# Expert-choice routing on Trainium2: scales spread through memory, the eight largest found chunk by chunk, table rows in another order

## The chip, the cores and the metric

The kernel runs on one core of a Trainium2 chip. The core has five engines that run side by side: TensorE (PE in the profile; PEld is its weight load), VectorE (DVE), ScalarE (ACT), GpSimd (POOL) and SyncE (SP), which only issues DMAs here. The metric is the device time of one execution in microseconds. Ten runs of the kernel before gave a median of 6127.88 us (6120.04 to 6132.37).

## The reference, cut to what matters

The kernel computes a whole small vision model: four layers, each with a convolution-like block and a feed-forward block, on an activation of 4 images x 128 channels x 64 x 64 pixels. The change is in the feed-forward block that layers 1 and 2 share, a mixture of experts in which each of 64 experts chooses 8 of the 4096 tokens of an image:

```python
t = _to_tokens(x)                                  # 4 images, 4096 tokens, 128 channels
t = t + _L1_ffn_ref(_ln_t(t), ...)                 # the norm is over the channels of a token

logits = jnp.einsum('bsd,ed->bse', x, gate_w) + gate_b
probs = jax.nn.softmax(logits, axis=1)             # over the tokens
vals, idx = jax.lax.top_k(probs.transpose(0, 2, 1), K)      # K = 8, for each image and expert
gathered = jnp.take_along_axis(x, flat_idx[:, :, None], axis=1)
pooled = jnp.einsum('bked,bke->bed', gathered, topv)
h = gelu(h @ weight1); out = h @ weight2           # per expert, on the pooled row
outputs = outputs.at[..., flat_idx].add(weighted)  # back to the chosen tokens
```

## The kernel before

The activation stays in on-chip memory as `xs`, channels on the 128 partitions and tokens along the free dimension, in chunks of 512 tokens (eight chunks an image). The function `expert_choice` runs once for layer 1 and once for layer 2. It handles the four images as two pairs; a pair fills the 128 partitions of the logits (64 experts of each image). Its first half, which the change touches, is the selection:

- `stat(p, j)` (L1313, L1315, L1323): a product with the centring matrix, its square on ACT, and for each four chunks products that add up the variances into one bank `pv`, one row per chunk. `scales` and `inverted` (L1336, L1340) make 1/sqrt of them in one tile `rstd`: 16 useful rows of 512 tokens, a row for each chunk of the pair.
- `turn_scales` (L1346, L1348) turns these rows, so that a token's scale stands beside the token's row; the result is `turned`.
- `logits(p, c)` (L1357 to L1365): PE spreads the chunk's scale over the 128 partitions by a product with a selection matrix `own`, ACT copies it out, PE makes the logits with the centred gate, DVE multiplies the two, ACT adds the gate's bias. The result is the chunk's part of `chosen[p]`, 128 x 4096.
- `largest(p)` (L1398 to L1407): DVE finds the eight largest of the 4096 (MAX8), then their places (FIND_INDEX8), adds the image's offset and makes whole numbers of them.
- `rows(b, c)` (L1387 to L1392): four transposes turn 512 tokens into rows, ACT copies them into one of five buffers `xts`, adds the scale as one more column (L1390), and SP writes the buffer to a table in memory. The buffer's number is `(b * NCH + c) % len(xts)`, and the copy into a buffer waits until the write from it is done.
- `exponentials(p, c)`, `denominators(p)` (L1415, L1419, L1420): the softmax's sums.
- `ask(p, j)` (L1425): POOL asks by indirect DMA for the j-th chosen row of each expert from the pair's table.
- `pool(p)` (L1434 to L1452): diagonal matrices with the shares on DVE, eight products that pool the rows, a copy on ACT, the centring product, and a copy to `pooled`.

After that come the experts: 16 groups of four, whose weights (2 MB a group) are loaded by SP in order, four groups early, the rest as buffers come free. L1518 is their first product.

In this half PE, ACT, DVE and POOL work their instructions in the order of the program text (the pool of the stage is opened with `tc.manual_schedule(engines=ORDERED)`); only SP's DMAs are ordered by the scheduler. So an instruction that waits holds all that stand behind it on its engine. The order is written at the end of the stage:

```python
for c in range(NCH):
    logits(1, c)
    if c < 4:
        exponentials(0, c + 4)
    for n in (2 * c, 2 * c + 1):
        rows(1 + n // NCH, n % NCH)
denominators(0)
largest(1)
for c in range(NCH):
    rows(3, c)
    ask(0, c)
```

Of the kernel before, what the change touches and what calls it, by code (L numbers as in the profile page):

```python
# [28 lines left out]
P = 128  # L29
B, H, W = 4, 64, 64  # L30
N = H * W
CH = 512
NCH = N // CH
# [1182 lines left out]
def expert_choice(net, layer):  # L1216
# [24 lines left out]
    with ExitStack() as ctx:  # L1241
        dram = ctx.enter_context(tc.tile_pool(name="moe_dram", bufs=1, space=bass.MemoryType.DRAM))
        tables = [dram.tile([2 * N, ROW], F32, name=f"moe_table{p}") for p in range(PAIRS)]
        keep = ctx.enter_context(tc.tile_pool(name="moe", bufs=1))
        early = ctx.enter_context(tc.tile_pool(name="moe_w", bufs=EARLY))
        gate = keep.tile([D, E], F32, name="moe_gate")
# [18 lines left out]
        totals = [keep.tile([P, 1], F32, name=f"moe_total{i}") for i in range(PAIRS)]  # L1265
        cgate = keep.tile([D, E], F32, name="moe_cgate")

        behind = keep.tile([P, 1], F32, name="moe_behind")
        nc.gpsimd.memset(behind[0:E], 0.0)
        nc.gpsimd.memset(behind[E:P], float(N))  # L1270

        tops = {}
        negs = [keep.tile([P, 1], F32, name=f"moe_neg{p}") for p in range(PAIRS)]
# [22 lines left out]
        with (  # L1296
# [5 lines left out]
            def bank(tag, name):  # L1302
                return ps.tile([P, CH], F32, name=f"moe_{name}", tag=tag, bufs={"a": 3, "b": 3}.get(tag, 1))
# [28 lines left out]

            def scales(p):
                variances(p, 3)
                rstd = sb.tile([P, CH], F32, name="moe_rstd", tag="moe_rstd")
                nc.scalar.activation(rstd, stats[p][0], AF.Sqrt, bias=net.eps[1e-5])  # L1336
                rstds[p] = rstd

            def inverted(p):
                nc.vector.reciprocal(rstds[p], rstds[p])  # L1340

            def turn_scales(p):

                pt = bank("a", "pr")
                for k in range(4):
                    nc.tensor.transpose(pt[:, k * P : (k + 1) * P], rstds[p][:, k * P : (k + 1) * P], net.ident)  # L1346
                turned[p] = sb.tile([P, 2, NCH, 4], F32, name="moe_turned", tag="moe_turned")
                nc.vector.tensor_copy(  # L1348
                    turned[p].rearrange("p i (a q) k -> p k q (i a)", q=4),
                    pt.rearrange("p (k q r) -> p k q r", q=4, r=32)[:, :, :, 0:4],  # L1350
                )

            def logits(p, c):
                pb, pl = bank("b", "rb"), bank("a", "pl")
                q = c % 4
                rows = slice(32 * q, 32 * q + 32)
                nc.tensor.matmul(pb, own[rows, c // 4, :], rstds[p][rows], start=True, stop=True)  # L1357
                for i in range(2):
                    nc.tensor.matmul(
                        pl[i * E : (i + 1) * E], cgate, net.chunk(2 * p + i, c), start=True, stop=True  # L1360
                    )
                lg = chosen[p][:, c * CH : (c + 1) * CH]
                nc.scalar.copy(lg, pb)
                nc.vector.tensor_mul(lg, lg, pl)
                nc.scalar.activation(lg, lg, AF.Identity, bias=gbias)  # L1365

            xts = [sb.tile([P, 4, ROW], F32, name=f"moe_xt{i}", bufs=1) for i in range(5)]
            for t in xts:
                nc.gpsimd.memset(t[:, :, P:ROW], 0.0)

            own = sb.tile([P, 2, 2 * E], F32, name="moe_own", bufs=1)
            for q in range(4):
                group = slice(32 * q, 32 * q + 32)
                for r in range(2):
                    for i in range(2):
                        at = 32 * q + 2 * i + r
                        nc.gpsimd.tensor_copy(
                            own[group, r, i * E : (i + 1) * E], net.ident[group, at : at + 1].to_broadcast([32, E])
                        )

            def rows(b, c):

                p, i = divmod(b, 2)
                pt = bank("b", "pt")
                for t in range(4):
                    tok = slice((4 * c + t) * P, (4 * c + t + 1) * P)
                    nc.tensor.transpose(pt[:, t * P : (t + 1) * P], net.xs[:, b, tok], net.ident)  # L1387
                xt = xts[(b * NCH + c) % len(xts)]
                nc.scalar.copy(xt[:, :, 0:P], pt.rearrange("p (t d) -> p t d", d=P))
                nc.scalar.copy(xt[:, :, P], turned[p][:, i, c, :])  # L1390
# [3 lines left out]
            places, shares, asked = {}, {}, {}  # L1394

            def largest(p):
                top = keep.tile([P, K], F32, name=f"moe_top{p}")
                nc.vector.max(out=top, in_=chosen[p])  # L1398
                tops[p] = top
                place = sb.tile([P, K], U32, name="moe_place", tag="moe_place")  # L1400
                nc.vector.max_index(out=place, in_max=top, in_values=chosen[p])
                row = sb.tile([P, K], F32, name="moe_row", tag="moe_row")
                nc.vector.tensor_copy(row, place)
                nc.vector.tensor_scalar(row, row, behind, None, op0=ALU.add)
                places[p] = sb.tile([P, K], I32, name="moe_idx", tag="moe_idx")
                nc.vector.tensor_copy(places[p], row)
                nc.vector.tensor_scalar_mul(negs[p], top[:, 0:1], -1.0)  # L1407

            sums = [sb.tile([P, NCH], F32, name=f"moe_sums{p}", bufs=1) for p in range(PAIRS)]

            def exponentials(p, c):

                sq = sb.tile([P, CH], F32, name="moe_sq", tag="moe_sq", bufs=5)
                lg = chosen[p][:, c * CH : (c + 1) * CH]
                nc.scalar.activation(sq, lg, AF.Exp, bias=negs[p], accum_out=sums[p][:, c : c + 1])  # L1415

            def denominators(p):
                shares[p] = sb.tile([P, K], F32, name="moe_share", tag="moe_share")
                nc.scalar.activation(shares[p], tops[p], AF.Exp, bias=negs[p])  # L1419
                nc.vector.tensor_reduce(totals[p], sums[p], AX.X, ALU.add)  # L1420

            def ask(p, j):
                if j == 0:
                    asked[p] = sb.tile([P, K, ROW], F32, name="moe_asked", tag="moe_asked")
                nc.gpsimd.indirect_dma_start(  # L1425
                    out=asked[p][:, j, :],
                    out_offset=None,
                    in_=tables[p],
                    in_offset=bass.IndirectOffsetOnAxis(ap=places[p][:, j : j + 1], axis=0),
                )  # L1430
# [26 lines left out]
                stat(0, j)  # L1457
            scales(0)
            inverted(0)
            for j in range(5):  # L1460
                stat(1, j)
            turn_scales(0)
            pg = bank("b", "pg")
            nc.tensor.matmul(pg[:, 0:E], net.cent, gate, start=True, stop=True)
            nc.vector.tensor_copy(cgate, pg[:, 0:E])
            for c in range(NCH):
                logits(0, c)
            largest(0)
            for j in range(5, 2 * NCH):
                stat(1, j)  # L1470
                if j % 3 == 0:
                    rows(0, j // 3 - 2)
            scales(1)
            inverted(1)
            for c in range(4, NCH):
                rows(0, c)
                exponentials(0, c - 4)
            turn_scales(1)
            for c in range(NCH):
                logits(1, c)  # L1480
                if c < 4:
                    exponentials(0, c + 4)
                for n in (2 * c, 2 * c + 1):
                    rows(1 + n // NCH, n % NCH)
            denominators(0)
            largest(1)
            for c in range(NCH):
                rows(3, c)
                ask(0, c)
# [5 lines left out]
            pool(0)  # L1495

            pg = bank("b", "pb").rearrange("p (i c) -> p i c", i=NH)
            for i in range(NH):
# [1084 lines left out]
```

## Time and profile before

| what | value |
|---|---|
| median of ten runs | 6127.88 us |
| the profiled execution's own time | 6131.45 us |
| its span, first to last instruction | 6129.6 us |
| busy: PE, DVE, ACT, POOL | 5707.2, 4356.0, 3405.8, 2066.2 us |
| mean granted TensorE clock | 0.97 |
| bytes moved by DMA, mean rate | 836.40 MB, 136 GB/s |
| selection in layer 1, from the end of the first pair's variances to the experts' first product | 2500.70 to 2601.71 us |
| the same in layer 2 | 2970.14 to 3070.48 us |

Times in the views are microseconds from the start of the span unless they are marked ns. A timeline line gives start, duration, engine, source line, operation, output and inputs; where the engine stood idle before, a bracket at its end gives for how long and what released it. SPq is SP's queue of DMA issues.

### The profile page before, as it was taken

What the parts mean: (1) busy time and instruction counts of PE and PEld (TensorE: products, weight loads), DVE (VectorE), ACT (ScalarE), POOL (GpSimd) and SP (SyncE); (2) the same over time, 40 slices, a digit from 0 to 9 for tenths busy, and PEclk for the clock granted to TensorE, in tenths of its full rate; (3) what the DMA queues carried; (4) which work ended last, traced back from release to release, by engine and by line L of the source; (5) the groups of instructions that cost most, each with busy time, mean ns of one, the idle gap of its engine ahead of it and who ended that gap; (6) DMA issues with size and microseconds to landing.
All of it is one profiled execution on the core that took longest, in us unless ns stands there. A gap on an engine that the chain in (4) does not pass through costs nothing. (4 is left out here: it accounts for less than half of the span.)

```text
span 6129.6 us, 97925 instructions
## 1 busy us (share of the span) xinstructions
PE 5707.2 (93%) x39892; PEld 2243.1 (37%) x39923; DVE 4356.0 (71%) x4707; ACT 3405.8 (56%) x4256; POOL 2066.2 (34%) x2015
## 2 busy tenths in 40 slices
PE   8999999879999988789879999999999999999799
PEld 2222222446766766333333222322232223222233
DVE  6888887456767666357347778777877778888666
ACT  4444444332323222420428889888888888999421
POOL 3889896027777777100101111111111111111000
PEclk9999999989999999889989999999999999999899
DMA  6443431068777877440365566556665666666200
GB/s 212 97 84 78 97 77 41 1 189 251 225 242 231 257 215 211 149 162 0 125 234 125 131 149 146 126 130 144 142 135 123 140 140 138 132 136 131 62 23 28
DMA packets 291041, 836.40 MB, mean 136 GB/s; under 512 B 43356, under 2 KB 117596, under 8 KB 244492
## 3 DMA queue, kind: packets, MB, share of 16 engines
q0 software_dynamic: 109568, 505.75, 34.5%
q1 hardware_dynamic: 181004, 324.17, 18.2%
q8 instruction: 321, 5.26, 0.3%
q14 instruction: 148, 1.21, 0.1%
HBM read 416.71 MB, written 111.10 MB: 86 GB/s over the span
## 5 line engine op out<-in xcount | busy, mean ns | idle before, releaser
L1989 ACT ACTIVATE att_ex<-att_sc,att_shift 128x1024 f32<-128x1024 f32 x2048 | 2155.6, 1111 | 327.9 <-PE att_sc L1985 151.1
L2020 DVE TENSOR_TENSOR att_dve<-att_dve,att_ex 128x2048 f32<-128x2048 f32 x704 | 1633.8, 2321 | 348.8 <-ACT att_ex L1989 325.9
L1985 PE MATMUL att_sc<-att_q,att_k 32*128 32x512 f32 x8192 | 1283.8, 644 | 16.3 <-ACT att_ex L1989 16.3
L2001 PE MATMUL att_pv<-att_ex,att_vals 128*32 128x512 f32 x8192 | 1098.9, 608 | 6.6 <-ACT att_hidden L2027 5.6
L969 POOL DMA_INDIRECT dcn_g<-dcn_table,dcn_idx x896 | 850.2, 949 | 368.4 <-issue 156.3
L412 DVE SCALAR_TENSOR_TENSOR inv_prod<-inv_pk,bspan,inv_seen 128x512 f32<-128x512 f32 (+1 forms) x1120 | 774.6, 743 | 141.2 <-PE inv_pk L399 140.8
L410 POOL TENSOR_TENSOR inv_prod<-inv_seen,inv_prod 128x512 f32<-128x512 f32 (+1 forms) x672 | 837.6, 1274 | 95.0 <-ACT inv_prod L409 95.0
L2018 POOL DMA_DIRECT2D att_dma<-att_ex x224 | 192.5, 859 | 1912.8 <-ACT att_ex L1989 1681.1
L409 ACT ACTIVATE inv_prod<-inv_pk,bspan 128x512 f32<-128x512 f32 (+1 forms) x672 | 436.1, 682 | 504.7 <-PE inv_pk L399 494.9
L977 DVE TENSOR_TENSOR dcn_g<-dcn_g,dcn_near_w 128x1024 f32<-128x1024 f32 x448 | 540.0, 1216 | 217.7 <-DMA dcn_g<-dcn_table,dcn_idx 199.8
L1985 PEld LDWEIGHTS att_sc<-att_q,att_k 32*128 32x128 f32 x8192 | 423.5, 184 | 662.7 <-issue 436.6
L986 PE MATMUL dcn_pt<-ident,dcn_g 128*128 128x128 f32 x3584 | 479.3, 278 | 63.1 <-DVE dcn_g L977 39.0
L399 PE MATMUL inv_pk<-inv_red,wtap 32*96 32x512 f32 (+1 forms) x3584 | 511.8, 636 | 7.3 <-DVE wtap L377 7.3
L986 PEld LDWEIGHTS dcn_pt<-ident,dcn_g 128*128 128x128 f32 x3584 | 419.9, 143 | 222.4 <-issue 132.1
L421 PE MATMUL inv_out<-inv_prod,inv_fold 96*32 96x512 f32 (+1 forms) x3584 | 478.5, 606 | 8.5 <-DVE xs L429 8.5
L2001 PEld LDWEIGHTS att_pv<-att_ex,att_vals 128*32 128x32 f32 x8192 | 161.7, 108 | 793.6 <-issue 757.2
L1092 ACT COPY dcn_st<-dcn_pt 128x512 f32<-128x512 f32 x224 | 129.6, 579 | 307.8 <-PE dcn_pt L986 300.4
L399 PEld LDWEIGHTS inv_pk<-inv_red,wtap 32*96 32x96 f32 (+1 forms) x3584 | 131.6, 170 | 386.4 <-DVE inv_prod L412 362.7
L1099 PE MATMUL dcn_out<-dcn_st,dcn_wk 128*128 128x512 f32 x448 | 237.6, 613 | 24.1 <-DVE xs L1107 21.7
L2487 PE MATMUL top_po<-top_xg,top_we 128*128 128x512 f32 x512 | 233.5, 599 | 0.0
L1005 ACT ACTIVATE dcn_fold<-dcn_pf,dcn_turn 128x256 f32<-128x256 f32 x128 | 60.1, 473 | 300.5 <-PE dcn_pf L1001 300.5
L2468 DVE TENSOR_TENSOR top_xg<-top_d,top_pw 128x512 f32<-128x512 f32 x256 | 158.2, 679 | 63.0 <-PE top_pw L2458 63.0
(433 smaller groups left out, 5320.8 us busy)
## 6 DMA issues: line engine op xcount, KB each, us to landing
att_dma<-att_ex POOLq DMA_DIRECT2D x224, 1024.0 KB, 7.1
inv_seen<-inv_image SPq DMA_DIRECT2D x256, 266.0 KB
moe_w<-in_L_ffn_weight SPq DMA_DIRECT2D x64, 1024.0 KB
dcn_table<-dcn_xt SPq DMA_DIRECT2D x64, 512.0 KB
att_dma<-att_ex SPq DMA_DIRECT2D x32, 1024.0 KB
att_dve<-att_dma POOLq DMA_DIRECT2D x32, 1024.0 KB, 9.0
moe_table<-moe_xt SPq DMA_DIRECT2D x64, 288.0 KB
dcn_g<-dcn_table,dcn_idx POOLq DMA_INDIRECT x896, 3.8
```

Of the source, the lines that this page charges most:

```text
L399: nc.tensor.matmul(pk[0:m], wtap[half][rg, i, blk], red[rg, h * CH : (h + 1) * CH], start=True, stop=True)
L409: nc.scalar.activation(prod[0:m, h], pk[0:m], AF.Identity, bias=by)
L410: nc.gpsimd.tensor_mul(of, view, of)
L412: nc.vector.scalar_tensor_tensor(out=of, in0=as_shape(pk[0:m], of), scalar=by, in1=view, op0=ALU.add, op1=ALU.mult)
L421: nc.tensor.matmul(po[CR * blk : CR * (blk + 1), h, :], fold[0:m], prod[0:m, h, :], start=unit == 0, stop=unit == UNITS - 1,)
L969: nc.gpsimd.indirect_dma_start(out=g[:, t, :], out_offset=None, in_=rows, in_offset=bass.IndirectOffsetOnAxis(ap=idx[:, Q4 * c + i + t, k ...
L977: nc.vector.tensor_mul(near, near, by)
L986: nc.tensor.matmul(pt[0][:, (i + t) * P : (i + t + 1) * P], near[:, t, q, :], net.ident, is_transpose=True, start=i + t + q == 0, stop=i + ...
L1985: nc.tensor.matmul(pes[h // 2][:, h % 2, :], ks[r, t * P : (t + 1) * P], q[r], start=True, stop=True)
L1989: nc.scalar.activation(ex[:, 2 * two : 2 * two + 2, :], pes[two], AF.Exp, bias=shifts[g][:, two : two + 1],)
L2001: nc.tensor.matmul(block["pv"][r], vals[:, t, r], ex[:, h, :], start=t == 0, stop=t == NT - 1)
L2020: nc.vector.tensor_add(block[who], block[who], ex)
```

## The change

It changes only the selection half of `expert_choice`, so it acts twice in the kernel.

- The scales go to a small table in memory (`spread_scales`, four DMAs of four rows) and come back spread over 64 partitions, two DMAs a chunk (`way`), into three buffers; the next read is asked for when a chunk's logits are through. The selection matrix `own`, its products and ACT's copies go.
- The eight largest are found for each chunk of 512 as soon as its logits are there (`largest_of`), and `largest` chooses among the 64 candidates; their places are picked out by comparing 64 ordinal numbers with the eight positions.
- The scale's column of a table row is copied by POOL and no longer by ACT.
- The order is another one: the second pair's squares and the first rows run between the first pair's logits; rows of two images alternate; the first pair's asks stand ahead of the second pair's logits; the first pair is pooled before the second pair's exponentials.
- `rstd` and the buffer of asked rows (`asked`) exist once instead of twice.

```diff
-                rstd = sb.tile([P, CH], F32, name="moe_rstd", tag="moe_rstd")
+                rstd = sb.tile([P, CH], F32, name="moe_rstd", tag="moe_rstd", bufs=1)
...
+            def spread_scales(p):
+                for r in range(4):
+                    nc.sync.dma_start(spread[p][4 * r : 4 * r + 4, :], rstds[p][r:P:32])
+
+            def way(p, c):
+                by = ways[p, c] = sb.tile([P, CH], F32, name="moe_by", tag="moe_by", bufs=3)
+                for i in range(2):
+                    row = i * NCH + c
+                    nc.sync.dma_start(by[i * E : (i + 1) * E], spread[p][row : row + 1, :].to_broadcast([E, CH]))
...
             def logits(p, c):
-                pb, pl = bank("b", "rb"), bank("a", "pl")
-                q = c % 4
-                rows = slice(32 * q, 32 * q + 32)
-                nc.tensor.matmul(pb, own[rows, c // 4, :], rstds[p][rows], start=True, stop=True)
+                pl = bank("a", "pl")
...
-                nc.scalar.copy(lg, pb)
-                nc.vector.tensor_mul(lg, lg, pl)
+                nc.vector.tensor_mul(lg, ways.pop((p, c)), pl)
                 nc.scalar.activation(lg, lg, AF.Identity, bias=gbias)
+                if c + 3 < NCH:
+                    way(p, c + 3)
...
-                nc.scalar.copy(xt[:, :, P], turned[p][:, i, c, :])
+                nc.gpsimd.tensor_copy(xt[:, :, P], turned[p][:, i, c, :])
...
+            def largest_of(p, c):
+                lg = chosen[p][:, c * CH : (c + 1) * CH]
+                nc.vector.max(out=peaks[p][:, c, :], in_=lg)
+                nc.vector.max_index(out=spots[p][:, c, :], in_max=peaks[p][:, c, :], in_values=lg)
...
             def largest(p):
                 top = keep.tile([P, K], F32, name=f"moe_top{p}")
-                nc.vector.max(out=top, in_=chosen[p])
+                flat = peaks[p].rearrange("p c k -> p (c k)")
+                nc.vector.max(out=top, in_=flat)
                 tops[p] = top
+                nc.vector.tensor_scalar_mul(negs[p], top[:, 0:1], -1.0)
...
-                nc.vector.max_index(out=place, in_max=top, in_values=chosen[p])
+                nc.vector.max_index(out=place, in_max=top, in_values=flat)
+                at = sb.tile([P, K], F32, name="moe_at", tag="moe_at")
+                nc.vector.tensor_copy(at, place)
+                known = sb.tile([P, NCH, K], F32, name="moe_known", tag="moe_known")
+                nc.vector.tensor_copy(known, spots[p])
+                nc.vector.tensor_add(known, known, behind)
...
+                for j in range(K):
+                    nc.vector.scalar_tensor_tensor(
+                        out=found[:, j, :], in0=order, scalar=at[:, j : j + 1],
+                        in1=known.rearrange("p c k -> p (c k)"), op0=ALU.is_equal, op1=ALU.mult,
+                    )
                 row = sb.tile([P, K], F32, name="moe_row", tag="moe_row")
...
+                nc.vector.tensor_reduce(row, found, AX.X, ALU.add)
...
-                    asked[p] = sb.tile([P, K, ROW], F32, name="moe_asked", tag="moe_asked")
+                    asked[p] = sb.tile([P, K, ROW], F32, name="moe_asked", tag="moe_asked", bufs=1)
```

The order at the end of the stage, as it is after the change (from the first pair's logits to the second pair's asks):

```python
for c in range(NCH):
    logits(0, c)
    largest_of(0, c)
    stat(1, NCH + c)
    if c % 2:
        rows(0, c // 2)
scales(1)
inverted(1)
spread_scales(1)
for c in range(3):
    way(1, c)
largest(0)
for c in range(4, NCH):
    rows(0, c)
    rows(1, c - 4)
    exponentials(0, c - 4)
turn_scales(1)
for c in range(4, NCH):
    rows(1, c)
    rows(2, c - 4)
    exponentials(0, c)
denominators(0)
for j in range(K):
    ask(0, j)
for c in range(NCH):
    logits(1, c)
    largest_of(1, c)
    rows(3, c)
    if c < 4:
        rows(2, c + 4)
largest(1)
pool(0)
for c in range(NCH):
    exponentials(1, c)
denominators(1)
for j in range(K):
    ask(1, j)
```

More of the change, by code (lines that the diff above doesn't have):

```diff
@@ L1243, in expert_choice @@
         tables = [dram.tile([2 * N, ROW], F32, name=f"moe_table{p}") for p in range(PAIRS)]
+        spread = [dram.tile([2 * NCH, CH], F32, name=f"moe_spread{p}") for p in range(PAIRS)]
         keep = ctx.enter_context(tc.tile_pool(name="moe", bufs=1))
@@ L1266, in expert_choice @@
         cgate = keep.tile([D, E], F32, name="moe_cgate")
-        behind = keep.tile([P, 1], F32, name="moe_behind")
-        nc.gpsimd.memset(behind[0:E], 0.0)
-        nc.gpsimd.memset(behind[E:P], float(N))
+        behind = keep.tile([P, NCH, K], F32, name="moe_behind")
+        for c in range(NCH):
+            nc.gpsimd.memset(behind[0:E, c, :], float(c * CH))
+            nc.gpsimd.memset(behind[E:P, c, :], float(N + c * CH))
+        order = keep.tile([P, NCH * K], F32, name="moe_order")
+        for i in range(NCH * K):
+            nc.gpsimd.memset(order[:, i : i + 1], float(i))
         tops = {}
@@ L1351, in turn_scales @@
                 )
+            ways = {}
+            def spread_scales(p):
[6 more added lines that the diff above has]
+                    nc.sync.dma_start(by[i * E : (i + 1) * E], spread[p][row : row + 1, :].to_broadcast([E, CH]))
             def logits(p, c):
-                pb, pl = bank("b", "rb"), bank("a", "pl")
-                q = c % 4
-                rows = slice(32 * q, 32 * q + 32)
-                nc.tensor.matmul(pb, own[rows, c // 4, :], rstds[p][rows], start=True, stop=True)
+                pl = bank("a", "pl")
                 for i in range(2):
@@ L1369, in expert_choice @@
                 nc.gpsimd.memset(t[:, :, P:ROW], 0.0)
[L1371 to L1379, printed above, removed]
             def rows(b, c):
@@ L1394, in expert_choice @@
             places, shares, asked = {}, {}, {}
+            peaks = [sb.tile([P, NCH, K], F32, name=f"moe_peaks{p}", bufs=1) for p in range(PAIRS)]
+            spots = [sb.tile([P, NCH, K], U32, name=f"moe_spots{p}", bufs=1) for p in range(PAIRS)]
+            def largest_of(p, c):
+                lg = chosen[p][:, c * CH : (c + 1) * CH]
+                nc.vector.max(out=peaks[p][:, c, :], in_=lg)
+                nc.vector.max_index(out=spots[p][:, c, :], in_max=peaks[p][:, c, :], in_values=lg)
@@ new lines, in largest @@
+                at = sb.tile([P, K], F32, name="moe_at", tag="moe_at")
[3 more added lines that the diff above has]
+                nc.vector.tensor_add(known, known, behind)
+                found = sb.tile([P, CH], F32, name="moe_sq", tag="moe_sq", bufs=5)
+                found = found.rearrange("p (j k) -> p j k", j=K)
+                for j in range(K):
+                    nc.vector.scalar_tensor_tensor(
+                        out=found[:, j, :],
+                        in0=order,
+                        scalar=at[:, j : j + 1],
+                        in1=known.rearrange("p c k -> p (c k)"),
+                        op0=ALU.is_equal,
+                        op1=ALU.mult,
+                    )
@@ L1402, in largest @@
                 row = sb.tile([P, K], F32, name="moe_row", tag="moe_row")
-                nc.vector.tensor_copy(row, place)
-                nc.vector.tensor_scalar(row, row, behind, None, op0=ALU.add)
+                nc.vector.tensor_reduce(row, found, AX.X, ALU.add)
                 places[p] = sb.tile([P, K], I32, name="moe_idx", tag="moe_idx")
                 nc.vector.tensor_copy(places[p], row)
-                nc.vector.tensor_scalar_mul(negs[p], top[:, 0:1], -1.0)
             sums = [sb.tile([P, NCH], F32, name=f"moe_sums{p}", bufs=1) for p in range(PAIRS)]
@@ L1459, in expert_choice @@
             inverted(0)
-            for j in range(5):
+            spread_scales(0)
+            for c in range(3):
+                way(0, c)
+            pg = bank("b", "pg")
+            nc.tensor.matmul(pg[:, 0:E], net.cent, gate, start=True, stop=True)
+            nc.scalar.copy(cgate, pg[:, 0:E])
+            for j in range(NCH):
                 stat(1, j)
             turn_scales(0)
-            pg = bank("b", "pg")
-            nc.tensor.matmul(pg[:, 0:E], net.cent, gate, start=True, stop=True)
-            nc.vector.tensor_copy(cgate, pg[:, 0:E])
             for c in range(NCH):
                 logits(0, c)
[L1468 to L1472, printed above, removed]
+                largest_of(0, c)
+                stat(1, NCH + c)
+                if c % 2:
+                    rows(0, c // 2)
             scales(1)
             inverted(1)
+            spread_scales(1)
+            for c in range(3):
+                way(1, c)
+            largest(0)
             for c in range(4, NCH):
                 rows(0, c)
+                rows(1, c - 4)
                 exponentials(0, c - 4)
             turn_scales(1)
+            for c in range(4, NCH):
+                rows(1, c)
+                rows(2, c - 4)
+                exponentials(0, c)
+            denominators(0)
+            for j in range(K):
+                ask(0, j)
             for c in range(NCH):
                 logits(1, c)
+                largest_of(1, c)
+                rows(3, c)
                 if c < 4:
[L1482 to L1485, printed above, removed]
+                    rows(2, c + 4)
             largest(1)
-            for c in range(NCH):
-                rows(3, c)
-                ask(0, c)
+            pool(0)
             for c in range(NCH):
@@ L1494, in expert_choice @@
                 ask(1, j)
-            pool(0)
             pg = bank("b", "pb").rearrange("p (i c) -> p i c", i=NH)
```

## The prediction

> **What bounds the kernel now.** I read the page for the size of things, then the timeline of each engine over the two stretches that the change touches, then the busy time by stretch. On the page the mixture of experts is small. Its selection part runs twice, between the end of the first pair's variance products (2500.70 us in layer 1, 2970.14 us in layer 2) and the first product of the experts (2601.71 and 3070.48 us): 101.0 and 100.3 us. The experts behind it wait for weights (L1518 stood 22.4 us for moe_w) whose buffers come free only when their products run, so a microsecond lost or won here is one of the kernel. Below, t counts from 2970.14.
>
> The stretches of layer 2 (columns: window, then its length, then busy us and instructions of PE, its weight loads, DVE, ACT, POOL, then granted clock, DMA share, GB/s):
>
> ```profile
> 2970.10:2980.00 9.90, 9.90 (x31) 3.78 (x30) 4.87 (x5) 5.45 (x9) 0.00 (x0) 1.00 0.78 286
> 2980.00:3012.10 32.10, 29.95 (x122) 10.63 (x120) 17.24 (x15) 20.79 (x41) 0.00 (x0) 1.00 0.15 46
> 3012.10:3042.00 29.90, 28.04 (x120) 12.25 (x120) 5.91 (x12) 23.74 (x63) 5.70 (x6) 0.94 0.59 171
> 3042.00:3051.70 9.70, 4.37 (x28) 2.93 (x28) 9.52 (x7) 6.43 (x22) 1.88 (x2) 0.99 1.07 299
> 3051.70:3070.50 18.80, 8.91 (x44) 7.96 (x47) 7.42 (x26) 6.46 (x19) 7.54 (x8) 0.64 0.25 63
> ```
>
> PE is full up to 3042; then DVE alone (9.52 of 9.70: the two scans of 4096), then a chain over ACT, POOL, DVE and PE. The edges of these parts, from the timelines of PE and DVE:
>
> ```profile
> 3012.20 0.66 PE L1346 MATMUL moe_pr<-ident,moe_rstd 128*128 128x128 f32 x4 [2.25 <-DVE moe_rstd L1340]
> 3041.97 4.43 DVE L1398 MAX8 moe_top<-moe_chosen 128x8 f32<-128x4096 f32 x1 [0.72 <-ACT moe_chosen L1365]
> 3046.51 4.42 DVE L1401 FIND_INDEX8 moe_place<-moe_top,moe_chosen 128x8 uint32<-128x4096 f32 x1
> 3063.90 0.15 DVE L1434 RECIPROCAL moe_total<-moe_total 128x1 f32<-128x1 f32 x1
> 3070.48 1.90 PE L1518 MATMUL moe_ph<-moe_w,moe_pooled 128*4 128x512 f32 x16 [1.17 <-issue]
> ```
>
> Two more rows carry the prices. On ACT (layer 1), how long a table buffer is away: the copy into it ends with L1390 at 2573.77 and the next copy into the same buffer (five copies later) starts at 2576.67, 2.90 us; later, with writes crowded, 2576.27 to 2580.92, 4.65 us. On POOL, eight asks in a row start 1.25 us apart:
>
> ```profile
> 2573.57 0.20 ACT L1390 COPY moe_xt<-moe_turned 128x4 f32<-128x4 f32 x1
> 2576.04 0.23 ACT L1390 COPY moe_xt<-moe_turned 128x4 f32<-128x4 f32 x1
> 2576.67 0.58 ACT L1389 COPY moe_xt<-moe_pt 128x512 f32<-128x512 f32 x1 [0.40 <-DMA moe_table<-moe_xt]
> 2580.92 0.58 ACT L1389 COPY moe_xt<-moe_pt 128x512 f32<-128x512 f32 x1 [0.33 <-DMA moe_table<-moe_xt]
> ...
> 3035.88 0.94 POOL L1425 DMA_INDIRECT moe_asked<-moe_table,moe_idx  x1 [0.30 <-issue]
> 3037.13 0.94 POOL L1425 DMA_INDIRECT moe_asked<-moe_table,moe_idx  x1 [0.30 <-issue]
> ```
>
> And attention already spreads scales by way of memory, so the route has rows: reciprocal over at 3189.16 + 3.39 = 3192.55, two spread writes, the reads back, first use at 3197.60, 5.05 us in all.
>
> ```profile
> 3192.61 1.19 SPq L1869 DMA_DIRECT2D att_spread<-att_scale  x2
> 3194.36 4.87 SPq L1874 DMA_DIRECT2D att_by<-att_spread  x3
> ...
> 3197.60 0.69 DVE L1893 TENSOR_TENSOR att_k<-att_by,att_sc 128x512 f32<-128x512 f32 x1 [4.27 <-DMA att_by<-att_spread]
> ```
>
> **The change, part by part (layer 2).** Removed: 16 spreading products a layer (half of the 2.06 us that a chunk of logits takes on PE), their copies on ACT (0.58 each), 32 small ACT copies (0.20, about 0.1 each when pipelined) and the two scans of 4096. Added: 32 small POOL copies, 32 scans of 512, a merge of 17 short DVE steps per pair, 40 DMAs on SP. The 80 small memsets on POOL (0.09 to 0.15 each, up to 12 us) lie under the 19 us of variances at the front, where POOL did 3.98; without that cover they would delay the first table write, which nobody awaits. The sum goes by five steps.
>
> *First scales.* The first reciprocal ends at t 4.2 (2971.03 + 3.35). With four spread writes instead of two (0.6 each) the attention route gives first use at 4.2 + 5.05 + 1.2 = 10.5; the weights' traffic (DMA share 0.78 up to 2980) ends near t 7.4 and may push it to 12. PE meanwhile does eight squares' products, one variance set, the turn and the first logits: 10.1. I take 11.5 (before: 2977.51, t 7.4).
>
> *First pair, now paced by DVE.* Per chunk, in DVE's order: multiply 0.69, ACT's bias 0.72 in between, largest of 512, 0.09 of loading, index of 512, hand-overs 0.06. No scan of 512 is in the trace: by proportion 4.43/8 = 0.55, by the nearest row of that length (L2046, TENSOR_REDUCE of 512, 0.686) 0.69; I take 0.69, since a short instruction pays its start. Sum 2.94, eight times 23.5, so t 35.0; the second reciprocal, behind the last square, variance and root, ends at 39.0. Before: 3012.14, t 42.0. Won: 3.0. The second pair's squares and four row blocks ride along on PE (19.4 us) and ACT.
>
> *Middle: 16 row blocks and 8 exponentials.* ACT's own work is 16 x 0.48 + 8 x 0.72 + a table load 1.28 = 14.7. But the buffer is chosen by (8b + c) mod 5 and the blocks of two batches are now interleaved: 4 3, 0 4, 1 0, 2 1, 2 1, 3 2, 4 3, 0 4. From the third pair on the second copy mostly takes the buffer that the first copy of the pair before has filled. That buffer is away for copy 0.58 + POOL's column 0.27 (wake 0.08 by L410 behind L409, work 0.19 by L1263) + 2.90 = 3.75; with 1.2 of ACT's work between, two pairs take 4.95: 2.5 a pair, 20.0 for eight. And SP first issues four spreads and six reads of the second pair (4.3 to 6 us, and waiting for the spread's landing, 1.75) while the write of row block (0,5) stands behind them: about 3.5 once. t 39.0 + 20.0 + 3.5 = 62.5.
>
> *Second pair.* Chunks 0 and 1 go at 2.94. Then the new wait: POOL, which now writes the scale column, has the eight asks of pair 0 ahead of the columns of blocks (3,0) and (2,4). The asks wait for the last table write of that pair (copied near 60.5, landed 64.3) and take 8 x 1.25 = 10.0: t 74.3. Then two columns 0.46, the two writes 2.90 and 1.05 for the one behind (288 KB at the 276 GB/s of 2570 to 2580): 78.7. Block (3,1) needs that very buffer, so ACT stands still, and behind it on ACT block (2,5) and the bias of chunk 2, for which DVE waits: it starts at 79.7 instead of 69.3. Chunks 3, 4 and 5 have the same reuse one copy apart: 0.58 + 0.27 + 2.90 + 0.55 (half a place behind the other write) + 0.48 = 4.8 each, the last without the 0.48: 93.6. Two more at 2.94; the last bias ends at 100.2 (before: 3041.94, t 71.8).
>
> *Tail.* Scans 1.5, then the merge: two scans of 64 (0.25 and 0.35), eight selections and four casts or adds of 8 to 64 elements (0.2 each by 128x64 rows), a reduction of 512 (0.69), about 4.0: places at 105.7. That is 5.5 against 9.7 before. Pool 0 stands now ahead of the exponentials: 4.8 (3057.55 to 3062.36), 110.5, then exponentials and shares 5.9, 116.4; pool 1 could end 6.3 later (3063.90 to 3070.48, less 0.3 of waiting), 122.7. But there is one buffer for the asked rows now, so the asks of pair 1 wait for pool 0's products: start 110.4, the eighth 8.75 later, usable 2.65 after its start (3064.49 to L1439 at 3067.14), 121.8, and 3.3 from there to the first product (3067.14 to 3070.48). End: 125.1.
>
> So 125.1 against 100.3, +24.8; layer 1 has no weights' traffic at that point (0.00 DMA share after 2500), one less: 23.8. Sum 48.6. The profiled execution took 6131.45 (span 6129.6): 6180.0; the median of the runs lies 3.6 below it, so **6176**.
>
> [...]
>
> **Rivals.** *Only the asks hold* (writes come back within ACT's own work): middle 14.7 to t 53.7, asks over at 65.7, bias of chunk 2 at 71.1, five more chunks 14.7, tail 24.9: 111.4, +11 a layer, 6150. Against it: 2.90 is the shortest round trip in the trace and three copies last 2.2 at most. *The writes hide and the asks stand clear* (not slower): 39.0 + 14.7 + 22.2 + 24.9 = 100.8, and with scans of 0.55, 4.5 less: 6120 to 6129. It decides when a buffer is back within 1.9 us of ACT's hand-over; before, with five copies between uses, ACT waited only 3.1 us over both layers, which speaks for it as far as order is left alone. *Crowded writes* (4.65 as in the last rows of layer 1): 1.75 more, four times over in the middle and four in the second pair, 14 a layer: 6204. Against it: the copies are further apart than the 0.6 of that row.
>
> **How the numbers follow.** Forecast 0.70, only the asks 0.10, hidden 0.10, crowded 0.10. Unknowns downward: round trip 2.50 (fastest ask) -6, scans -7, SP's order -7, issue 0.94 alone -10, hardly all at once; upward a round trip of 3.9 +16, SP and POOL +6. That makes 6146 to 6198, and the range ends there. A measurement tells about 0.2% (12 us). Hidden splits into faster 0.06 and same 0.04; a forecast that shrinks to under 12 us adds 0.02: slower 0.88.
>
> **What would show it.** Right: ACT idle before the table copies for the table's DMA, tens of us where it was 3.1; one gap of about 10 us a layer while POOL asks; multiplies of the second pair near 4.8 apart behind it; the first pair's 2.9 apart. Wrong: ACT's copies close together, or the stage near 100 us. A reading of scales that comes late (DVE waiting for it after the first chunk) would mean that I priced the spread too low.

## The result and the profile after

The kernel after takes 6176.9 us (median of 8 runs, 6171.33 to 6182.07), the kernel before 6128.36 (28 runs): a ratio of 1.0081, 95% interval 1.0072 to 1.009. The forecast was 6176. The profiled execution took 6179.34 us with a span of 6177.5, 47.9 more than before. The stage of layer 2 now starts at 2992.5; t below counts from there.

The stretches of the kernel after in layer 2 (columns as before: window, length, busy us and instructions of PE, its weight loads, DVE, ACT and POOL, granted clock, DMA share, GB/s). They are the front, the first pair, the middle, the second pair and the tail:

```profile
2992.50:3006.50 14.00, 12.11 (x41) 4.45 (x40) 3.62 (x2) 5.56 (x10) 0.68 (x5) 1.00 0.71 253
3006.50:3033.70 27.20, 22.41 (x98) 7.84 (x98) 19.78 (x34) 14.58 (x24) 0.61 (x4) 1.00 0.38 115
3033.70:3058.60 24.90, 14.36 (x62) 9.76 (x64) 3.87 (x21) 13.29 (x31) 1.82 (x12) 0.59 0.63 188
3058.60:3094.30 35.70, 14.35 (x68) 5.82 (x64) 15.08 (x30) 11.18 (x21) 9.39 (x20) 0.81 0.54 156
3094.30:3118.70 24.40, 9.62 (x40) 8.07 (x41) 12.11 (x46) 6.88 (x21) 7.68 (x8) 0.64 0.15 38
```

Before, PE was busy for 93% of the time and more up to t 72. Now there are 60.6 us in the middle and the second pair in which no engine is busy for more than 58% of its time (PE 14.36 of 24.90, DVE 15.08 of 35.70). Time goes to waits. The timelines of ACT and POOL name them:

```profile
3043.41 0.58 ACT L1394 COPY moe_xt<-moe_pt 128x512 f32<-128x512 f32 x1 [6.41 <-DMA moe_table<-moe_xt]
3050.84 0.58 ACT L1394 COPY moe_xt<-moe_pt 128x512 f32<-128x512 f32 x1 [2.50 <-DMA moe_table<-moe_xt]
3073.73 1.07 ACT L1394 COPY moe_xt<-moe_pt 128x512 f32<-128x512 f32 x2 [10.84 <-DMA moe_table<-moe_xt]
3083.00 1.07 ACT L1394 COPY moe_xt<-moe_pt 128x512 f32<-128x512 f32 x2 [3.20 <-DMA moe_table<-moe_xt]
3060.22 0.98 POOL L1454 DMA_INDIRECT moe_asked<-moe_table,moe_idx  x1 [2.86 <-DMA moe_table<-moe_xt]
3068.99 0.95 POOL L1454 DMA_INDIRECT moe_asked<-moe_table,moe_idx  x1 [0.30 <-issue]
3069.94 0.32 POOL L1395 COPY moe_xt<-moe_turned 128x4 f32<-128x4 f32 x2
3104.39 0.97 POOL L1454 DMA_INDIRECT moe_asked<-moe_table,moe_idx  x1 [16.42 <-PE moe_acc L1476]
```

ACT's copies into the table buffers wait for the writes from those buffers: 59.1 us in 22 waits over both layers, 3.1 in 8 before. These lines are from the two kernels' lists of waits, before and after (total in us, times, longest):

```profile
ACT moe_xt L1389 <- DMA moe_table<-moe_xt: 3.1, 8, 0.5
ACT moe_xt L1394 <- DMA moe_table<-moe_xt: 59.1, 22, 10.8
```

The longest wait, 10.84, begins while POOL works off the eight asks (3060.22 to 3069.94). The two scale columns that stood behind the asks come at 3069.94, their writes after them, and ACT's copy at 3073.73. The last line is the other new wait: the second pair's asks stood until the first pair's products had read the only buffer of asked rows.

The scales' way and the pace of the first pair, from the timelines of SP and DVE:

```profile
2996.83 2.14 SPq L1362 DMA_DIRECT2D moe_spread<-moe_rstd  x4
3001.07 10.12 SPq L1368 DMA_DIRECT2D moe_by<-moe_spread  x10
3006.53 0.69 DVE L1377 TENSOR_TENSOR moe_chosen<-moe_by,moe_pl 128x512 f32<-128x512 f32 x1 [4.68 <-DMA moe_by<-moe_spread]
3009.41 0.67 DVE L1377 TENSOR_TENSOR moe_chosen<-moe_by,moe_pl 128x512 f32<-128x512 f32 x1
3036.01 3.67 SPq L1368 DMA_DIRECT2D moe_by<-moe_spread  x6
```

DVE waits for a scale once, at the start (4.68 us); after that the chunks come 2.87 apart. And the tail:

```profile
3094.37 0.70 DVE L1406 MAX8 moe_peaks<-moe_chosen 128x8 f32<-128x512 f32 x1 [0.79 <-ACT moe_chosen L1378]
3095.78 0.21 DVE L1412 MAX8 moe_top<-moe_peaks 128x8 f32<-128x64 f32 x1
3099.39 0.17 DVE L1436 CAST moe_idx<-moe_row 128x8 int32<-128x8 f32 x1
3110.50 0.15 DVE L1463 RECIPROCAL moe_total<-moe_total 128x1 f32<-128x1 f32 x1
3118.72 1.89 PE L1557 MATMUL moe_ph<-moe_w,moe_pooled 128*4 128x512 f32 x8 [1.17 <-issue]
```

From the last bias to the places it takes 5.2 us where the two scans of 4096 took 9.7, so this part of the change does what it says.

### The profile page after: what moved, and what is told of

The parts are those of the page before. It is cut to its first block, busy times and chain, and to the rows that moved or that the text cites. A ratio compares the mean times of both kernels' runs of the same rounds, so it can differ in the third digit from the quotient of the medians.

```text
span 6177.5 us, 98159 instructions
## 1 busy us (share of the span) xinstructions
PE 5696.3 (92%) x39828; PEld 2247.3 (36%) x39859; DVE 4375.6 (71%) x4841; ACT 3383.1 (55%) x4162; POOL 2077.5 (34%) x2203
## 3 DMA queue, kind: packets, MB, share of 16 engines
q1 hardware_dynamic: 186252, 332.70, 18.5%
## 5 line engine op out<-in xcount | busy, mean ns | idle before, releaser
L1025 DVE TENSOR_TENSOR dcn_square<-dcn_hx,dcn_by 128x512 f32<-128x512 f32 x192 | 130.0, 677 | 102.9 <-PE dcn_pt L986 66.4
```

## The experiments

The theory was the prediction's: short reuse of the table buffers and the asks ahead of the scale columns make the loss, not the scales' way through memory or the scans by chunk. Each kernel was timed in five rounds beside the kernel before. The runs were on more than one chip: the kernel before took 6125.4 beside the first four, 6325.4 and 6325.1 beside the next seven, and 6131.0 beside the last. On the two slower chips (one for e5t, e6, e7 and e9, one for e8, e10 and e11) nearly all of the time is lost before these stages (the selection of layer 1 starts near 2690 us instead of 2500), so the kernels are compared by their ratio and by the length of the stage, counted here from ACT's root of the first pair's variances to the first moe_ph product. The ratio is worked out over all runs of both kernels; the quotient of the medians differs from it by up to 0.0007. A stage is that of one profiled execution, and the kernel before was profiled on a faster chip alone. The intervals of e2, e3, e4 and e6 overlap with that of the kernel after, so what these four gain is read from the stage and its waits.

| kernel | ratio to before | interval | stage, layer 1 | stage, layer 2 |
|---|---|---|---|---|
| before | 1 | | 100.7 | 100.2 |
| after | 1.0081 | 1.0072 to 1.009 | 123.9 | 126.1 |
| e1_ring: buffers in turn | 1.0049 | 1.0035 to 1.0063 | 111.1 | 114.2 |
| e2_asks: one ask a chunk | 1.0071 | 1.0057 to 1.0085 | 116.0 | 119.8 |
| e3_col: column on ACT | 1.0070 | 1.0056 to 1.0084 | 118.8 | 119.7 |
| e4_asked2: second buffer of asked rows | 1.0070 | 1.0056 to 1.0083 | 121.1 | 123.8 |
| e5t_all: e1, e2, e4 and the tail's order | 0.9997 | 0.9987 to 1.0006 | 101.5 | 103.7 |
| e6_products: after, spread by products | 1.0068 | 1.0054 to 1.0082 | 123.7 | 123.1 |
| e7_scans: before, scans by chunk | 1.0021 | 1.0012 to 1.003 | 108.9 | 109.3 |
| e8_spread: before, spread by memory | 0.9990 | 0.9981 to 0.9999 | 98.0 | 101.4 |
| e9_order: the change in a new order | 0.9953 | 0.9939 to 0.9966 | 87.5 | 87.8 |
| e10_oneread: after, one read a chunk | 1.0227 | 1.0213 to 1.0241 | 170.3 | 172.2 |
| e11_best: e9 with one read a chunk | 1.0154 | 1.014 to 1.0168 | 151.0 | 150.1 |
| e12_products: e9, spread by products | 1.0001 | 0.9991 to 1.001 | 99.8 | 100.6 |

**e1_ring.** The buffer is taken by a running counter.

```diff
-                xt = xts[(b * NCH + c) % len(xts)]
+                xt = xts[next(turns) % len(xts)]     # turns = iter(range(...))
```

> The kernel after, but the table buffers are taken in turn by a running counter, so that five copies lie between two uses of a buffer instead of one to three. Nothing else moves. Theory (the reuse of the table buffers holds ScalarE, and GpSimd's asks lengthen it): ScalarE's copies wait for the table's DMA no longer in the middle part, the 6.4 us stall behind SP's queue is covered, and of the 10.8 us stall behind the asks about half stays, because four copies can run ahead; the selection stage falls from 126.2 to about 114 us in layer 2, the total from 6177 to about 6152. Rival one (the spread by way of memory and SP's queue are the cost): the first scales still come at 14 us and the stall at SP stays, total 6170 to 6177. Rival two (the scans by chunk and the merge on VectorE are the cost): no change, 6177.

6153.64 us against 6125.41. ACT's waits for the table fell from 59.1 us to 25.4. The stall behind SP's queue, which was expected to be covered, is 3.67, and these are the two long waits that are left in layer 2 (ACT's timeline):

```profile
3023.98 0.58 ACT L1395 COPY moe_xt<-moe_pt 128x512 f32<-128x512 f32 x1 [3.67 <-DMA moe_table<-moe_xt]
3049.74 0.58 ACT L1395 COPY moe_xt<-moe_pt 128x512 f32<-128x512 f32 x1 [8.10 <-DMA moe_table<-moe_xt]
```

The reuse distance (how many copies lie between two uses of the same buffer) is the largest single cost: 12.8 and 11.9 us of the stage. The wait behind the asks is 8.1, more than the half that was expected, but it comes one chunk later, and the chunks behind it are 2.87 apart instead of 3.9 to 4.9.

**e2_asks and e3_col.** The same wait taken apart from the other side, by moving the asks and by moving the column.

```diff
-            for j in range(K):
-                ask(0, j)
             for c in range(NCH):
                 logits(1, c)
...
                     rows(2, c + 4)
+                ask(0, c)
```

> The kernel after, but the eight asks of the first pair are spread over the second pair's loop, one at the end of each chunk behind its table rows, as the kernel before had them. Theory: the scale columns of the third pair of copies no longer stand behind 10 us of asks, so the stall of 10.8 us shrinks to a wait for the landing of the last table write (about 4) and each chunk pays about 1.25 us more on GpSimd; the first pair's pooling comes a little later. Stage about 122 us instead of 126.2, total about 6168. If the asks are not what holds ScalarE at that place (the writes alone do), the stall stays and the total is 6177 or, as every chunk then waits for its ask, a few us more.

```diff
-                nc.gpsimd.tensor_copy(xt[:, :, P], turned[p][:, i, c, :])
+                nc.scalar.copy(xt[:, :, P], turned[p][:, i, c, :])
```

> The kernel after, but the scale column of a table row is copied by ScalarE again and not by GpSimd. Theory: the columns then never stand behind the asks, the stall of 10.8 us shrinks to the usual wait for a buffer (3 to 4), while ScalarE has 32 small copies more (0.1 to 0.2 each, part of them in time in which it waits anyway); stage about 122 us, total about 6168. Rival (the asks delay the table writes in memory or in the DMA queues and not on GpSimd): the stall stays at about 10 us, total 6177 to 6183.

6168.9 and 6172.47 us. The wait that had been 10.84 is 2.92 in e2_asks (first line) and 3.67 in e3_col (second line), where the asks stand in one block as before:

```profile
3061.34 1.08 ACT L1394 COPY moe_xt<-moe_pt 128x512 f32<-128x512 f32 x2 [2.92 <-DMA moe_table<-moe_xt]
...
3064.70 0.59 ACT L1394 COPY moe_xt<-moe_pt 128x512 f32<-128x512 f32 x1 [3.67 <-DMA moe_table<-moe_xt]
```

So it was POOL's order that held the columns, and not the asks' traffic: with the column on another engine, the same asks at the same place no longer hold it. The stage is 5 to 8 us shorter.

**e4_asked2.** The second pair's asked rows go into two table buffers that are free by then.

```diff
+            def row_at(p, j):
+                return asked[p][:, j, :] if p == 0 else xts[(2, 3)[j // 4]][:, j % 4, :]
...
-                    out=asked[p][:, j, :],
+                    out=row_at(p, j),
```

> The kernel after, but the asked rows of the second pair land in two of the table buffers that are free by then, so that its asks need not wait for the first pair's products. Theory: the asks start about 4.5 us earlier (when the places are there and the last table write has landed), the diagonals of the second pair no longer wait for them, and the end is set by the exponentials on ScalarE, which stay behind the first pair's pooling: 2 us a layer, total about 6173. If the single buffer of asked rows were a main cost, the whole 4.5 us a layer would be won: 6168. If the exponentials alone bind, nothing: 6177.

6170.24 us, the stage 2.8 and 2.3 shorter: a small term, as expected, near the 2 us a layer of the theory; the 4.5 a layer of a single buffer that is a main cost did not come.

**e5t_all.** All three, and the second pair's exponentials ahead of `pool(0)`.

```diff
-            pool(0)
             for c in range(NCH):
                 exponentials(1, c)
             denominators(1)
+            pool(0)
```

> The kernel after with all that the first theory blames taken out: table buffers in turn, the first pair's asks one at the end of each chunk of the second pair, the second pair's asked rows in two free table buffers, and the second pair's exponentials on ScalarE ahead of the first pair's pooling. Spread by memory, scans by chunk, merge and GpSimd's columns stay. Theory (buffers, the place of the asks and the tail make up the whole loss): 24 us less a layer, stage about 102.5 as in the kernel before (100.2 to 100.7), total about 6129. Rivals: the spread by memory or the scans by chunk hold part of it: total 6140 to 6155, with the rest to be seen in VectorE's waits.

A ratio of 0.9997: the loss is gone, with the spread by memory, the scans by chunk and POOL's columns still in place. ACT's waits for the table are 10.0 us in 10 waits over both layers. Layer 2 keeps 3.5 us over the stage of before, layer 1 0.8; 2.3 of the difference is the first scale, which comes at 13.5 there and at 11.2 in layer 1.

**e6_products.** After, with the products, ACT's copies and `own` of before.

```diff
+                nc.tensor.matmul(pb, own[ways, c // 4, :], rstds[p][ways], start=True, stop=True)
...
-                nc.vector.tensor_mul(lg, ways.pop((p, c)), pl)
+                nc.scalar.copy(lg, pb)
+                nc.vector.tensor_mul(lg, lg, pl)
```

> The kernel after, but the scales are spread by products again, with ScalarE's copies, as before; the scans by chunk, the order, the buffers and GpSimd's columns stay. Theory: the first pair starts some 4 us earlier and SP's queue no longer holds the row blocks, but the first pair stays paced by VectorE and the stalls at the table buffers and the asks stay; 4 to 5 us a layer, total about 6168. Rival (the way through memory is the main cost): total near 6130.

Ratio 1.0068, the stage only 0.2 and 3.0 shorter. The first scale is used at 11.0 and 11.1, and not 4 us earlier than in the kernel after (11.4 and 13.9): with the new order eight of the second pair's squares stand ahead of it on PE, where the kernel before has five. ACT's timeline in layer 2 shows what SP's queue had cost and what it had not:

```profile
3234.12 0.58 ACT L1393 COPY moe_xt<-moe_pt 128x512 f32<-128x512 f32 x1 [0.92 <-DMA moe_table<-moe_xt]
3262.38 1.07 ACT L1393 COPY moe_xt<-moe_pt 128x512 f32<-128x512 f32 x2 [8.02 <-DMA moe_table<-moe_xt]
```

The first long wait is 0.92 where it was 6.41; the one behind the asks is shorter but stays (8.02, it was 10.84). Against these 5.5 us stands a longer first pair: with products and copies the second reciprocal ends at 43.6 in layer 2 and 43.5 in layer 1, in the kernel after at 41.1 and 38.6.

**e7_scans and e8_spread.** One part each, in the kernel before. Both have one buffer for the scales, e8 also the asked rows of e4, to make room. The scan stands right behind its chunk's logits:

```diff
                 logits(0, c)
+                largest_of(0, c)
```

> The kernel before with one part of the change alone: the eight largest found for each chunk and merged, behind each chunk's logits (and one buffer for the scales, to make room). Products, order, table buffers and columns are those of before. Theory: the first pair is paced by VectorE (2.87 a chunk instead of 2.06, 6 us later), the long scans go from the tail, but the tail is set by the last table write and the asks behind it, so little of that is won: about 4 us a layer more, total about 6136. Rival (the scans and the merge are the main cost of the change): 20 us a layer more, 6170. If the long scans of 4096 set the tail of before, it gets faster: 6115.

```diff
-                nc.tensor.matmul(pb, own[rows, c // 4, :], rstds[p][rows], start=True, stop=True)
...
-                nc.scalar.copy(lg, pb)
-                nc.vector.tensor_mul(lg, lg, pl)
+                nc.vector.tensor_mul(lg, ways.pop((p, c)), pl)
```

> The kernel before with one part of the change alone: the scales spread by way of memory instead of by products (one buffer for the scales, and the second pair's asked rows in table buffers, to make room). Long scans, order and columns are those of before. Theory: the first scale comes at 12 to 14 us instead of 7.3, but each chunk then costs TensorE one product and ScalarE one copy less, so the first pair is through at about the same time and the second pair's loop is a few us shorter: 0 to 3 us a layer won, total 6120 to 6128. Rival (the way through memory is a main cost of the change): the 5 to 7 us of the later start stay, total 6138 to 6142; if SP's queue holds the table writes too, up to 6155.

The scans alone cost 0.21%, more than expected: the stage is 8.2 and 9.1 us longer instead of 4. About 5 are the first pair's pace. For the rest, ACT stood ahead of its last row copies (3.48 us in layer 2, 1.35 and 1.30 in layer 1), and the profile names no releaser; that part stays open. The spread alone is at the edge of what the runs can tell: 0.1% faster, with an interval that ends at 0.9999, the stage 2.7 us shorter in layer 1 and 1.2 longer in layer 2. The start is 3 and 6 us later, but each chunk is rid of a product and a copy, and the second pair's multiplies come 2.6 us apart on the average in layer 2 instead of 3.5.

**e9_order.** All parts of the change; new are only the order and the asked rows of e4. With the rows of one image at a time the old formula for the buffer takes them in turn as well.

```python
for j in range(6): stat(1, j)
turn_scales(0)
for j in range(6, 10): stat(1, j)
some_rows(4)                                   # the next four of (b, c), in order
for c in range(NCH):
    logits(0, c)
    if c > 0: largest_of(0, c - 1)
    if c == 4: inverted(1); spread_scales(1)
    if 0 < c < 4: stat(1, 2 * c + 8); stat(1, 2 * c + 9)
    if c == 3: scales(1)
    if c > 4: way(1, c - 5)
    some_rows(0 if c in (2, 5) else 2)
turn_scales(1); largest_of(0, NCH - 1)
for c in range(NCH):
    logits(1, c)
    if c > 0: largest_of(1, c - 1)
    if c == 1: largest(0)
    some_rows(2)
    if c > 0: exponentials(0, c - 1); ask(0, c - 1)
```

After that come the last scan, exponential and ask, `largest(1)`, the exponentials of the second pair, its asks, and only then `pool(0)` and `pool(1)`.

> All parts of the change (spread by memory, scans by chunk, merge, GpSimd's columns) with the table buffers in turn, the second pair's asked rows in table buffers and a new order: the second pair's squares are through by the third chunk of the first pair, so that its reciprocal comes near 26 us; row blocks go two to a chunk through both pairs; a chunk's scans stand behind the next chunk's multiply; one ask of the first pair a chunk; the exponentials of the second pair ahead of the first pair's pooling. Theory: VectorE becomes the bound (14 us to the first scale, 16 chunks of about 2.2, a reciprocal 3.4, two merges of 3.8), the last bias near 62 us and the stage about 85 us, 15 less than before: total about 6098, faster than both kernels. Rival (a way through memory of 14 us and scans by chunk cannot be hidden): stage 100 or more, 6128 or more.

Ratio 0.9953: 28 us of 6325, faster than both kernels. Its stretches in layer 2 (front, first pair, second pair, tail):

```profile
3144.60:3159.10 14.50, 14.50 (x63) 6.46 (x64) 3.62 (x2) 8.76 (x16) 0.68 (x5) 1.00 0.70 251
3159.10:3188.30 29.20, 24.72 (x113) 10.57 (x114) 19.48 (x35) 15.65 (x27) 2.27 (x12) 0.94 0.65 190
3188.30:3210.60 22.30, 17.53 (x92) 8.70 (x92) 18.38 (x46) 17.49 (x35) 7.94 (x19) 0.92 1.02 288
3210.60:3232.40 21.80, 10.17 (x42) 7.96 (x43) 12.54 (x47) 9.52 (x27) 10.28 (x13) 0.61 0.38 99
```

PE is now full while the first scale is on its way, there is no middle, and in the second pair three engines are busy for 78 to 82% of the time. The first scale still comes at 14.5; it is covered.

**e10_oneread and e11_best.** One transfer brings a chunk's scales to both halves of the partitions.

```diff
-                for i in range(2):
-                    row = i * NCH + c
-                    nc.sync.dma_start(by[i * E : (i + 1) * E], spread[p][row : row + 1, :].to_broadcast([E, CH]))
+                pair = spread[p].rearrange("(i c) t -> c i t", i=2)[c]
+                nc.sync.dma_start(by, pair.unsqueeze(1).to_broadcast([2, E, CH]))
```

> The kernel after, but a chunk's scales are read back by one transfer for both halves of the partitions instead of two; nothing else moves. Theory: SP's queue holds the row block behind three reads instead of six, so the 6.4 us stall in the middle falls by 1.2 to 1.8 us and the first scale may come up to 1 us earlier; the rest (buffers, asks) stays: 1 to 3 us a layer, total about 6173. Rival one: a transfer over 128 partitions lands later than two over 64, so that the first pair waits: 0 to 5 us slower, 6177 to 6187. Rival two (SP's queue is the main cost): 6 us a layer and more, 6165 or less.

> The kernel with the new order (all parts of the change, the second pair's squares early, rows two to a chunk, scans one chunk behind, one ask a chunk), with one read of the scales a chunk instead of two. Theory: VectorE and TensorE are the bound, so little more is to be won: stage 85 to 88 us, a ratio to the kernel before of 0.994 to 0.995, near 6095. If the reads of two halves hold the second pair's multiplies (two of them waited 0.3 us for them), 1 us a layer more.

All of it wrong but for the sign of one rival: 1.0227 and 1.0154, some 92 and 127 us slower than the same kernels with two reads (the ratios' differences, 0.0146 and 0.0201, of 6325). In e10_oneread DVE's multiplies come 5.27 us apart in layer 1 (2.87 in the kernel after), for DVE waits for each read; two of them:

```profile
2717.51 0.69 DVE L1376 TENSOR_TENSOR moe_chosen<-moe_by,moe_pl 128x512 f32<-128x512 f32 x1 [2.30 <-DMA moe_by<-moe_spread]
2722.80 0.69 DVE L1376 TENSOR_TENSOR moe_chosen<-moe_by,moe_pl 128x512 f32<-128x512 f32 x1 [2.31 <-DMA moe_by<-moe_spread]
```

The last section has the rates of these reads.

**e12_products.** The new order with the products of before (and two buffers for the scales).

```diff
-                rstd = sb.tile([P, CH], F32, name="moe_rstd", tag="moe_rstd", bufs=1)
+                rstd = sb.tile([P, CH], F32, name="moe_rstd", tag="moe_rstd")
```

> The new order (second pair's squares early, rows two to a chunk, scans one chunk behind, one ask a chunk), but with the scales spread by products and ScalarE's copies again, and two buffers for the scales; everything else as in the run of the new order. Theory (the spread by memory pays in this order, because it takes 16 products and 16 copies from TensorE and ScalarE, which then bound the second pair): the first scale waits for the squares that stand ahead of it (t about 16), the second pair's chunks come 3.7 apart instead of 2.5, the stage takes about 100 us instead of 87.5, the ratio to the kernel before is about 1.000. Rival (the gain of the new order is the order alone, and the way of the scales does not matter): stage 86 to 90, ratio 0.995 to 0.996.

Ratio 1.0001, stage 99.8 and 100.6: the gain of e9 is not the order alone. The stretch of the second pair in layer 2:

```profile
3014.40:3042.80 28.40, 25.88 (x106) 11.63 (x105) 17.08 (x44) 20.76 (x41) 10.17 (x21) 0.88 0.54 159
```

TensorE is busy for 91% of it, and DVE's multiplies wait for PE's logits or for ACT's copies of the scale (1.53 to 2.40 us at six of the eight chunks), where in e9 the same work took 22.3 us. In this order the products and copies that the spread by memory takes away are worth 12.3 and 12.8 us a layer.

## Why the prediction was right, step by step

The sum of the two layers was 48.6; the stages grew by 23.1 and 25.9, 49.0, measured as the prediction counted them, and the span by 47.9. In layer 2, the step, the forecast and the trace:

| step (t) | forecast | measured |
|---|---|---|
| first scale used | 11.5 | 14.0 |
| first pair, per chunk | 2.94 | 2.87 |
| second reciprocal ends | 39.0 | 41.2 |
| middle ends | 62.5 | 66.1 |
| first ask, end of the asks | 64.3, 74.3 | 67.7, 77.4 |
| bias of chunk 2 of the second pair | 79.7 | 82.2 |
| last bias ends | 100.2 | 101.8 |
| places | 105.7 | 107.0 |
| second pair's asks | 110.4 | 111.9 |
| stage ends | 125.1 | 126.2 |

Three terms were mis-sized, and they offset each other: that the end of the stage came within 1.1 us is in part luck. *The first scales*: 2.5 late in layer 2, while in layer 1, without the weights' traffic, it was 11.6. So the route worked out from attention's rows (10.5) was 1.1 short. The other 2.4, where 1 was allowed, is the difference between the layers: with 253 GB/s at the front (the first stretch above) SP issued the first read 4.2 us after the first spread, in layer 1, where the traffic was 64 GB/s, 2.3 us. That the traffic makes the difference is read from these two layers; no run took it away. Hence the first pair won 0.8 and not 3.0. *SP's queue*: one wait of 6.41 where 3.5 stood; SP was busy with the second pair's spread and reads from 3033.76 to 3039.68, and the table writes came behind all of it. e6_products, which has no such transfers, shows 0.92 there. *The pairs of the middle* then took 18.5 (24.9 less 6.4) instead of 20.0, because part of their work ran earlier: the first pair's two copies start at 3030.24 and 3031.56 and the table load of 1.28 us at 3032.16, all before the second reciprocal ends at 3033.73. Behind the long wait the pairs came 2.75 us apart (3043.41 to 3057.14 for five), where the forecast had 2.5. The first of the three slow chunks behind the asks had another cause than the forecast's: by the profile ACT's copy waited 2.68 us for PE's transposes and not for a buffer; PE had stood 10.99 us behind ACT's long wait and had its own work to make up. Still, from the first ask on the intervals hold within 1 us: to the bias of chunk 2 14.5 (forecast 15.4), to the last bias 19.6 (20.5), to the places 5.2 (5.5), to the end 19.2 (19.4). e2_asks and e3_col confirm the price of the asks from two sides.

The rivals. *Only the asks hold* (6150) fell: e3_col takes the asks' hold away and still waits 2.5 to 3.7 a chunk for the table. *The writes hide* fell with ACT's 59.1 us. *Crowded writes* fell too: behind the asks the chunks of the second pair start 4.4, 4.9, 3.9 and 2.9 apart, where the forecast had 4.8 and crowding 1.75 more. The theory's own proof is e5t_all: with the buffers in turn, the asks apart and the tail turned round, ratio 0.9997.

Where the prediction was silent: it did not ask whether spread and scans would pay in an order made for them. All parts together do (e9_order, 0.9953), and the spread is needed for it (e12_products, 1.0001). Whether the scans by chunk pay in that order was not tried by itself; in the old order they cost 8.2 and 9.1 us a layer (e7_scans).

## What to carry to other kernels

A formula for a rotating buffer is right only for the order it was written for: when an order is changed, count the uses between two uses of the same buffer anew, against the time that the buffer is away. Before a small step is put on an idle engine, look at what stands ahead of it in that engine's queue: 0.2 us of work became a wait of 10.8, because 10 us of asks were ahead. And a change that loses need not consist of bad parts: take the new waits away one by one before the parts are given up.

## What the runs showed of the hardware

One transfer of 256 KB, repeated over the partitions, was slower than two of 128 KB: the multiplies that wait for it come 5.27 us apart, against 2.87 with two. In e10_oneread the read of a chunk has a source of 2 x 64 x 512 (the 64 by repetition) and goes to 128 partitions. This is a stretch of its first reads in layer 1:

```profile
2701.00:2711.00 10.00, 7.42 (x24) 1.71 (x24) 4.29 (x8) 2.88 (x5) 0.00 (x0) 0.83 0.14 51
```

Its DMA share is 0.14, about two of 16 engines (0.125), and the rate 51 GB/s: 256 KB at that rate are 5.1 us, nearly all of the 5.27 between two multiplies. In the packets of e10_oneread's trace, 12 to 14 of 2 KB start in most half microseconds, and one takes 84 ns (median), so that about two are under way at a time; in the kernel after, 36 to 58 start in each half microsecond of the first four microseconds of half reads in layer 1, one takes 84 ns (median) there as well, and the DMA share of these four (2511 to 2515) is 0.69, about eleven of 16 engines. By the median a packet takes as long in both; in the joined read fewer run side by side. Two reads to the two halves win by 92 and 127 us (e10_oneread, e11_best). Why the joined read has only about two packets under way is not shown: it was tried with this one pattern alone.
